# A two-layer graph kernel: where the bias of v, the scaling of the sums, layer 1's first sums and the key loads stand in the order of the work

## The chip, the cores and the metric

The kernel runs on one core of a Trainium2 chip. The metric is the device time in microseconds (us). TensorE (PE in the profile) multiplies matrices, PEld is its weight load, VectorE is DVE, ScalarE is ACT, GpSimd is POOL, and SyncE (SP) issues transfers. A waiting instruction holds up everything behind it on its engine or queue.

## The reference, cut to what matters

There are 16 graphs (b) of 1024 nodes with 256 features. Layer 0 is masked attention with 8 heads of 32; layer 1 is a graph layer whose scores come from the layer's own input `h` and one of four vectors, chosen by the value of `adj`.

```python
h = relu(layernorm(x))
Q, K, V = h @ Wq.T + bq, h @ Wk.T + bk, h @ Wv.T + bv           # by heads
attn = softmax(where(adj == 0, -inf, Q @ K.T * HD ** -0.5))     # per head
x = x + (attn @ V) @ Wo.T + bo
h = relu(layernorm(x))
e_k = leaky_relu((h * a_k) @ h.T, 0.2)                          # k = 0 .. 3
scores = where(adj == k + 1, e_k, -9e15)                        # the kind chosen per edge
x = x + softmax(scores) @ h
```

The adjacency is drawn as 0 or 1, so only `a_0` is used at run time; a general path for other values stands behind a test at the end of the program.

## The kernel before, in words

The main loop has 138 steps `s`; a step handles one tile of 128 nodes in several places at once. Attention of layer 0 works on tile `s` (`now`) and finishes tile `s - 1` (`was`); `gone` is the tile before. Normalising and projecting (`Piece`) runs nine tiles ahead: `piece_nxt` is loaded, `piece` is normed and turned, `piece_was` gets its keys, values and queries. Layer 1 (`Edges`) runs nine tiles behind: `edge` gets its scores, `edge_was` its sums and the store. Eight tiles make a graph; `t` is the tile within it, and between `t` = 7 and `t` = 0 the graph turns: the eight key tiles `k0` to `k7` (512 KB each) are loaded anew.

Each step runs over `h` = 0 to 7, and the order of the instructions on every engine is the order written in the program; no scheduler moves them. Waits are set from the data: an instruction waits for those that wrote what it reads or that still use what it overwrites, kept by whole tile. For head `h` a step has:

- scores(h), L423: TensorE writes a 128x1024 tile into one of two PSUM places.
- max(h), L435: VectorE adds the mask and finds the row's extreme; exp(h), L443, on ScalarE follows, issued in turn `h + 1`.
- The transpose of the probabilities, issued in turn `h + 2`. Heads 2, 3, 6, 7: TensorE, L543, with copies by ScalarE, L544. Heads 0, 1, 4, 5: VectorE turns blocks of 32x32 (L364, `turn_blocks`), then SP issues four transfers that put the blocks in place (L369, `place_blocks`). So head 1 is turned in turn h = 3, without TensorE.
- combine(0) in h = 7 and combine(1) in h = 3 of the next step, L478: TensorE sums the values over heads 0 to 3 and 4 to 7. combine(0) needs the transfers of heads 0 and 1, combine(1) those of heads 4 and 5.

The change and its surroundings touch these:

- L328 (`values`, h = 2) multiplies for v; L339 (`biased`) adds its bias on VectorE.
- L488 (`combined`): oT, the sums times the reciprocals, on VectorE. L493 (`output`, h = 4): TensorE multiplies oT by Wo. L499 (`residual`, h = 5): VectorE adds x.
- L231 (`piece.turn`, h = 5): TensorE transposes the next tile's h; L243 and L244 (`turned`): ScalarE copies it to SBUF. L261: the projections; L277 (`high`, ScalarE) and L282 (`split`, VectorE) read them in two parts and write `halves`, which go to DRAM as keys (kd, L309) and queries (qd, L303).
- L565: layer 1's scores; L579: their maximum on VectorE. L609 (`gather`): layer 1's sums, the first half in h = 5, the second in h = 6, from pT1, which comes through L364 and L369 as well. L618 (`store`): VectorE scales them and adds x, SP writes them out.
- L394 (`load`, h = 4): the adjacency of the tile after next, 512 KB, on the POOL queue. L403 makes the mask from it.
- L344 (`load_key`): one key tile, on the POOL queue. `KEY_STEPS` says where: entry i is the place of key i, 2h for the start of turn h and 2h + 1 for its end, in the step `t` = 7, and over 15 in the next one.

Two PSUM banks serve most of this. `sums_place` and `brief` lie in the first, `early` and `late` in the second. v's product, the query and key projections, `output` and the turn of h all go through `early` and `late`; since waits are kept by whole tile, a reader of one half of a bank also waits for the last write to the other half. So L277 for the queries waits for L231 if L231 was issued before it. combine, gather and `store` share `sums_place`, so combine(0) waits for L618.

SP issues its transfers one at a time and marks their ends in eight semaphores, its lanes, taken in turn: a transfer waits until the one before it on its lane, eight transfers earlier, has landed.

The lines that fix the order of keys and of h = 5 are these:

```python
KEY_STEPS = (6, 10, 13, 15, 18, 20, 22, 24)
...
(nc.sync, nc.gpsimd)[b > 0].dma_start(out=kt.bitcast(F32), in_=kds[b][c, ...])
```

Of the kernel before, what the change touches and what calls it, by code (L numbers as in the profile page):

```python
# [42 lines left out]
def gnn_kernel(  # L43
# [26 lines left out]
    LEAD = NT + 1  # L70


    KEY_STEPS = (6, 10, 13, 15, 18, 20, 22, 24)
    KEPT = LAG + 1

    const = ctx.enter_context(tc.tile_pool(name="const", bufs=1))
# [264 lines left out]
    def load_key(b, h):  # L341
        kt = keys.tile([P, N], F32R, tag=f"k{h}", name=f"k{h}_{b}")
        c, r = divmod(h, GROUP)
        (nc.sync, nc.gpsimd)[b > 0].dma_start(  # L344
            out=kt.bitcast(F32),
            in_=kds[b][c, r * HD : (r + 1) * HD].rearrange("d w u n -> (d w u) n"),
        )
        keysets.setdefault(b, {})[h] = kt
# [178 lines left out]
    def norms(tile_0, piece):  # L527

        both = [(a, x) for a, x in ((tile_0, tile_0 and tile_0.x1), (piece, piece and piece.x[:, 0, :])) if a]
        if both:  # L530
            mv = stats_place(len(both))
            for i, (_, xt) in enumerate(both):
                stats_of(xt, mv[:, i, :])
            r, shift = norm_of(mv)
            for i, (a, _) in enumerate(both):
                a.norm = r[:, i : i + 1], shift[:, i : i + 1]
# [151 lines left out]
    def attend_of(s):  # L688
        return Attend(*divmod(s, NT)) if 0 <= s < B * NT else None

    def edges_of(s):
        s -= LAG
        return Edges(*divmod(s, NT)) if 0 <= s < B * NT else None

    def piece_of(s):
        s += LEAD
        return Piece(*divmod(s, NT)) if s < B * NT else None

    with tc.manual_schedule():
        first = [Piece(0, 0, 4), Piece(0, 4, 4)]  # L700
        piece_was = Piece(1, 0)
# [23 lines left out]
        piece, edge, edge_was = piece_next, None, None  # L725
# [10 lines left out]
        for s in range(B * NT + LAG + 1):  # L736
            b, t = divmod(s, NT)

            def load_keys(h, end):
                if t == NT - 1 and b + 1 < B and 2 * h + end in KEY_STEPS:  # L740
                    load_key(b + 1, KEY_STEPS.index(2 * h + end))
                if t == 0 and 0 < b < B and 2 * (HEADS + h) + end in KEY_STEPS:
                    load_key(b, KEY_STEPS.index(2 * (HEADS + h) + end))

            nxt2, edge_nxt, piece_nxt = attend_of(s + 2), edges_of(s + 1), piece_of(s + 1)
            for h in range(HEADS):
                ending, eh = (now, h - 1) if h >= 1 else (was, HEADS - 1)
                turning, th = (now, h - 2) if h >= 2 else (was, HEADS + h - 2)

                load_keys(h, 0)  # L750


                if now:
                    now.scores(h)
                if h == 0 and piece_was:
                    piece_was.split()
                if h == 1 and piece_was:
                    piece_was.split()
                if h == 2 and edge:
                    edge.softmax_max()  # L760
                if h == 4 and piece_was:
                    piece_was.biased()
                if h == 4 and was:
                    was.combined()
                if h == 5:
                    if was:
                        was.residual()
                    norms(was, piece_nxt)
                if h == 6 and edge_was:
                    edge_was.gather(1)  # L770
                if h == 6 and piece_was:
                    piece_was.split()
                    piece_was.split()
                if now:
                    now.softmax_max(h)
                if h == 6 and edge_was:
                    edge_was.store()
                if h == 4 and edge:
                    edge.leak()


                if ending:
                    ending.softmax_exp(eh)

                if h == 1 and gone:
                    gone.turned_normed()


                if turning and th in BY_BLOCKS:
                    turning.turn_blocks(th)  # L790
                    turning.place_blocks(th)
                elif turning:
                    turning.turn(th, 0)
                    turning.turn(th, 1)


                if h == 0:
                    if piece_was:
                        piece_was.write_again()
                    if edge:  # L800
                        edge.score(0)
                    if gone:
                        gone.turn_normed()
                    if edge_was:
                        edge_was.turn_blocks()
                        edge_was.place_blocks()
                if h == 1:
                    if edge:
                        edge.score(1)
                    if was:  # L810
                        was.reciprocals()
                    if piece_nxt:
                        piece_nxt.load()
                    if piece_was:
                        piece_was.write_again()
                    if nxt:
                        nxt.load_queries()
                if h == 2:
                    if piece_was:
                        piece_was.values()  # L820
                    if was:
                        was.turn_reciprocals()
                        was.turned_reciprocals()
                        was.add_bias()
                    if edge_was:
                        edge_was.load_nodes()
                if h == 3:
                    if piece_was:
                        piece_was.project(1, 0)
                        piece_was.project(1, 1)  # L830
                    if was:
                        was.combine(1)
                    if nxt:
                        nxt.flag()
                        nxt.mask()
                if h == 4:
                    if was:
                        was.output()
                    if piece:
                        piece.normed()  # L840
                    if edge_nxt:
                        edge_nxt.prepare()
                    if nxt2:
                        nxt2.load()
                if h == 5:
                    if piece:
                        piece.turn()
                    if edge_was:
                        edge_was.gather(0)
                    if piece_was:  # L850
                        piece_was.high()
                        piece_was.high()
                    if piece:
                        piece.turned()
                if h == 6:
                    if edge:
                        edge.softmax_exp()
                    if was:
                        was.keep()
                    if now:  # L860
                        now.load_nodes()
                    if piece:
                        piece.project(0, 0)
                        piece.project(0, 1)
                if h == 7:
                    if now:
                        now.combine(0)
                    if piece_was:
                        piece_was.write_queries()
                    if piece:  # L870
                        piece.high()
                        piece.high()
                    if was:
                        was.normed()
                load_keys(h, 1)
            gone, was, now, nxt = was, now, nxt, nxt2
            edge_was, edge = edge, edge_nxt
            piece_was, piece = piece, piece_nxt
# [52 lines left out]
```

## Time and profile before

| what | value |
|---|---|
| median of 3 runs | 3343.77 us (3342.66 to 3351.56) |
| the profiled execution | 3346.32 us |
| its span, first to last instruction | 3344.4 us |
| mean granted TensorE clock | 0.985 |
| busy: TensorE, VectorE, ScalarE, GpSimd | 3091.6, 2809.3, 2466.1, 1726.9 us |
| TensorE waits for oT (L493 <- L488) | 75.6 us in 119 places |
| TensorE waits for the residual (L231 <- L499) | 26.6 us in 109 places |
| TensorE's combine waits for transfers of pT | 44.1 us in 32 places |
| transfers of pT, issue to landing, median | 3.5 us |
| key loads from POOL, issue to landing, median | 6.9 us |

A line of the timeline has the start in us, the length in us, the engine, the line of the kernel, the operation, out<-in, shapes and count; in brackets stands how long the engine was idle before it and what released it. "POOL L344 DMA_DIRECT2D" is the issue of a transfer on the POOL queue, not its movement. A line of stretches has the bounds, the length, busy time with the number of instructions of each engine, the granted TensorE clock, the mean busy share of the DMA engines and the GB/s they moved.

### The profile page before, as it was taken

The numbers are of one execution on the slowest core, as the hardware profiler recorded it, in microseconds if no ns is written. First come the engines' busy times: TensorE is split into PE (matmuls) and PEld (weight loads), VectorE is DVE, ScalarE is ACT, GpSimd is POOL, SyncE is SP. The second block draws the span as 40 slices with busy tenths as digits, with TensorE's granted clock in tenths as the row PEclk, the third lists the DMA queues.
The fourth block names the chain that finished last, engine by engine and source line by source line (L and its number), as shares of the span: only waits on it lengthen the run. The fifth ranks groups of instructions, "written<-read, shape, count | busy, mean of one in ns | idle before, by whom it ended". The sixth has DMA issues, their size and how long they took to land. (4 is left out here: it accounts for less than half of the span.)

```text
span 3344.4 us, 98033 instructions
## 1 busy us (share of the span) xinstructions
PE 3091.6 (92%) x36018; PEld 2217.5 (66%) x36018; DVE 2809.3 (84%) x5111; ACT 2466.1 (74%) x4829; POOL 1726.9 (52%) x3902
## 2 busy tenths in 40 slices
PE   4888999999999999999999999999999999999997
PEld 2766667676676666667667676666666676676653
DVE  2888889889888888888889888888888888888873
ACT  2887777777777777777777777777778778777750
POOL 2555555555555555555545555555555555555431
PEclk7999999999999999999999999999999999999999
DMA  5777787877878787787877878787787877877642
GB/s 191 227 229 247 214 263 228 256 223 227 252 221 267 212 244 241 213 257 231 256 218 229 255 223 269 217 246 239 215 266 222 260 224 231 249 228 236 192 136 70
DMA packets 747063, 762.93 MB, mean 228 GB/s; under 512 B 71280, under 2 KB 692080, under 8 KB 746576
## 3 DMA queue, kind: packets, MB, share of 16 engines
q1 hardware_dynamic: 678288, 542.21, 54.4%
q0 software_dynamic: 65088, 210.16, 20.1%
q8 instruction: 290, 4.75, 0.6%
q10 hardware_dynamic: 3200, 4.19, 0.3%
q14 instruction: 197, 1.61, 0.1%
HBM read 252.98 MB, written 167.77 MB: 126 GB/s over the span
## 5 line engine op out<-in xcount | busy, mean ns | idle before, releaser
L443 ACT ACTIVATE p<-p,nmx 128x1024 f32<-128x1024 f32 x1024 | 1178.0, 1150 | 308.4 <-DVE nmx L435 304.4
L435 DVE CUSTOM_DVE_ANT_0 p<-s,neg 128x1024 f32<-128x1024 f32 x1024 | 1235.1, 1206 | 140.4 <-issue 69.3
L423 PE MATMUL s<-k,qt 128*128 128x512 f32 x2048 | 794.5, 469 | 16.1 <-DVE nmx L435 9.5
L403 POOL TENSOR_SCALAR neg<-adj 128x1024 bf16<-128x1024 int32 x128 | 466.7, 3646 | 361.7 <-ACT neg L415 361.5
L544 ACT COPY pT<-trp 128x512 f32<-128x512 f32 x1024 | 544.3, 582 | 141.0 <-PE trp L543 125.0
L364 DVE STREAM_TRANSPOSE blocks<-p 128x1024 f32<-128x1024 f32 x512 | 633.2, 1237 | 0.1
L478 PE MATMUL acc<-pT,v 128*32 128x128 f32 x16384 | 529.1, 277 | 45.1 <-DMA pT<-blocks 44.1
L543 PE MATMUL trp<-ident,p 128*128 128x128 f32 x4096 | 530.9, 273 | 0.0
L478 PEld LDWEIGHTS acc<-pT,v 128*32 128x32 f32 x16384 | 448.8, 111 | 121.6 <-issue 94.9
L543 PEld LDWEIGHTS trp<-ident,p 128*128 128x128 f32 x4096 | 479.0, 140 | 69.4 <-issue 0.8
L609 PE MATMUL acc<-h,pT 128*32 128x256 f32 x8192 | 509.6, 383 | 12.2 <-DMA pT<-blocks 11.9
L565 PE MATMUL s<-h1T,ha 128*128 128x512 f32 x1024 | 481.6, 594 | 0.5 <-ACT h1T L522 0.5
L423 PEld LDWEIGHTS s<-k,qt 128*128 128x128 f32 x2048 | 329.3, 191 | 190.2 <-issue 154.7
L609 PEld LDWEIGHTS acc<-h,pT 128*32 128x32 f32 x8192 | 246.0, 110 | 227.7 <-issue 70.5
L462 POOL COPY wide<-rec 128x256 f32<-128x256 f32 x128 | 50.8, 397 | 556.1 <-DVE rec L460 556.1
L309 POOL DMA_DIRECT2D kd<-halves x240 | 168.3, 701 | 310.7 <-DVE halves L282 297.4
L579 DVE CUSTOM_DVE_ANT_0 sel<-s,neg 128x1024 f32<-128x1024 f32 x128 | 156.8, 1225 | 145.1 <-PE s L565 145.1
L565 PEld LDWEIGHTS s<-h1T,ha 128*128 128x128 f32 x1024 | 175.1, 190 | 129.7 <-issue 128.4
L493 PE MATMUL acc<-woT,oT 128*128 128x256 f32 x512 | 143.9, 403 | 75.6 <-DVE oT L488 75.6
L591 ACT ACTIVATE sel<-sel,nmx 128x1024 f32<-128x1024 f32 x128 | 145.2, 1134 | 69.3 <-DVE rec L616 64.0
L443 ACT ACTIVATION_READ_ACCUMULATOR p<-p,nmx 128x1 f32 x1024 | 193.2, 189 | 0.0
L472 ACT COPY recT<-acc 128x256 f32<-128x256 f32 x128 | 47.7, 373 | 178.1 <-PE acc L468 178.1
(106 smaller groups left out, 3986.7 us busy)
## 6 DMA issues: line engine op xcount, KB each, us to landing
pT<-blocks SPq DMA_DIRECT2D x2560, 128.0 KB, 3.5
qt<-qd SPq DMA_DIRECT2D x128, 512.0 KB, 5.6
adj<-in_adj POOLq DMA_DIRECT2D x127, 512.0 KB, 4.8
qd<-halves SPq DMA_DIRECT2D x240, 256.0 KB, 2.9
k<-kd POOLq DMA_DIRECT2D x120, 512.0 KB, 6.8
kd<-halves SPq DMA_DIRECT2D x240, 128.0 KB, 3.7
kd<-halves POOLq DMA_DIRECT2D x240, 128.0 KB, 3.6
xb<-in_x POOLq DMA_DIRECT2D x128, 128.0 KB, 2.6
```

What stands on the lines that cost most here:

```text
L309: queue.dma_start(out=kds[self.b][oc, :, :, twice, self.cols], in_=halves.rearrange("p (w n) -> p w n", w=2),)
L364: nc.vector.transpose(blocks.rearrange("p b j q -> p j b q"), p)
L403: nc.gpsimd.tensor_scalar(self.neg, self.adj, 0.0, MASKED, ALU.is_equal, ALU.mult)
L423: nc.tensor.matmul(self.ps[:, cols], lhsT=self.qt[:, h, :], rhs=keysets[self.b][h][:, cols], start=True, stop=True,)
L435: nc.vector.tensor_tensor_reduce(out=p, in0=sides[h in (3, 5, 7)], in1=self.neg, scale=-SCALE, scalar=FLOOR, op0=ALU.add, op1=ALU.min, acc ...
L443: nc.scalar.activation(p, p, AF.Exp, bias=nmx, scale=-1.0, accum_out=self.sums[:, h : h + 1])
L478: nc.tensor.matmul(sums_place[r * HD : (r + 1) * HD, g * P : (g + 1) * P], lhsT=vs[self.b][:, j, place_of(h) : place_of(h) + HD], rhs=self ...
L543: nc.tensor.transpose(tr[:, j, :], p[:, jj * P : (jj + 1) * P], ident)
L544: copy(pT[:, half * 4 : half * 4 + 4, :], tr)
L565: nc.tensor.matmul(self.e[:, cols], lhsT=self.ha[:, c, :], rhs=h1Ts[self.b][:, c, cols], start=(c == 0), stop=(c == NC - 1),)
L579: nc.vector.tensor_tensor_reduce(out=self.sel, in0=self.e, in1=masks[self.b, self.t], scale=-1.0, scalar=3e38, op0=ALU.add, op1=ALU.min, a ...
L609: nc.tensor.matmul(sums_place[a * HD : (a + 1) * HD, :], lhsT=self.pT[:, j, a], rhs=h1s[self.b][:, j, :], start=(j == 0), stop=(j == NT - 1),)
```

## The change

Four things move; no instruction is added or taken away.

1. The second, third, fourth and fifth key are loaded at other places: `KEY_STEPS` 10, 13, 15, 18 become 9, 10, 13, 16. Entry 9 (the end of h = 4) and entry 10 (the start of h = 5) have the same neighbours on the POOL queue for the key at that place.
2. project(1, .) and combine(1) are written ahead of the turn of head 1 in h = 3. Head 1's turn has nothing on TensorE, so TensorE's order stays.
3. The bias of v and oT go from h = 4, ahead of max(4), to h = 3, ahead of head 1's block transpose; on VectorE the order max(3), transpose, bias, oT, max(4) becomes max(3), bias, oT, transpose, max(4).
4. In h = 5 the first half of layer 1's sums (gather(0)) goes ahead of the turn of h on TensorE.

On POOL the order in the step `t` = 7 was: adjacency, key 1, the norm, xb, keys 2 and 3, kd, key 4. It becomes: adjacency, keys 1 and 2, the norm, xb, keys 3 and 4, kd. ScalarE's order and SP's order do not change.

```diff
-    KEY_STEPS = (6, 10, 13, 15, 18, 20, 22, 24)
+    KEY_STEPS = (6, 9, 10, 13, 16, 20, 22, 24)
...
-                if h == 4 and piece_was:
-                    piece_was.biased()
-                if h == 4 and was:
-                    was.combined()
                 if h == 5:
                     if was:
                         was.residual()
...
+                if h == 3:
+                    if piece_was:
+                        piece_was.project(1, 0)
+                        piece_was.project(1, 1)
+                    if was:
+                        was.combine(1)
+                    if piece_was:
+                        piece_was.biased()
+                    if was:
+                        was.combined()
                 if turning and th in BY_BLOCKS:
                     turning.turn_blocks(th)
                     turning.place_blocks(th)
...
                 if h == 3:
-                    if piece_was:
-                        piece_was.project(1, 0)
-                        piece_was.project(1, 1)
-                    if was:
-                        was.combine(1)
                     if nxt:
                         nxt.flag()
                         nxt.mask()
...
                 if h == 5:
+                    if edge_was:
+                        edge_was.gather(0)
                     if piece:
                         piece.turn()
-                    if edge_was:
-                        edge_was.gather(0)
                     if piece_was:
                         piece_was.high()
                         piece_was.high()
```

## The prediction

> **What bounds the kernel now.** I read the busy shares first, then the busy time by stretch, then the timeline of one ordinary step on all engines, and last the waits of TensorE and the POOL queue in a step where the graph turns.
>
> ```profile
> span 3344.4 us, 98033 instructions
> PE 3091.6 (92%) x36018; PEld 2217.5 (66%) x36018; DVE 2809.3 (84%) x5111; ACT 2466.1 (74%) x4829; POOL 1726.9 (52%) x3902
> ```
>
> No engine is full: TensorE leaves 8%, VectorE 16%. From the starts of scores(0) in the trace, 84 ordinary steps (t = 1 to 6, with layer 1 running) last 24.41 us in the median, 24.46 in the mean; the 14 steps with t = 7 last 26.9 in the mean, the steps with t = 0 after them 26.4. The stretches below are an ordinary step, a step t = 7 and the t = 0 after it (the last two columns are DMA share and GB/s).
>
> ```profile
> core 0: us, PE busy (x) PEld busy (x) DVE busy (x) ACT busy (x) POOL busy (x), PEclk, DMA share, GB/s
> 1498.98:1523.40 24.42, 23.59 (x286) 17.11 (x282) 21.89 (x41) 19.28 (x39) 12.95 (x29) 1.00 0.77 221
> ...
> 1419.93:1447.11 27.18, 23.99 (x286) 17.26 (x283) 22.75 (x42) 20.21 (x40) 16.32 (x35) 1.00 0.85 255
> 1447.11:1474.58 27.47, 24.87 (x285) 17.50 (x282) 22.25 (x40) 19.39 (x38) 14.15 (x32) 1.00 0.96 304
> ```
>
> TensorE is idle for 0.83 us of the ordinary 24.42, VectorE for 2.5: between them they form a ring, in which each waits for the other once or more. The timeline of that step shows where:
>
> ```profile
> 1505.62 1.23 DVE L579 CUSTOM_DVE_ANT_0 sel<-s,neg 128x1024 f32<-128x1024 f32 x1 [1.04 <-PE s L565]
> ...
> 1508.46 1.95 PE L478 MATMUL acc<-pT,v 128*32 128x128 f32 x64
> ...
> 1509.48 1.18 DVE L435 CUSTOM_DVE_ANT_0 p<-s,neg 128x1024 f32<-128x1024 f32 x1
> ...
> 1510.60 1.24 DVE L364 STREAM_TRANSPOSE blocks<-p 128x1024 f32<-128x1024 f32 x1
> ...
> 1511.77 0.38 DVE L339 TENSOR_TENSOR v<-acc,bv_t 128x256 f32<-128x256 f32 x1
> ...
> 1512.07 0.40 DVE L488 TENSOR_TENSOR oT<-acc,recT 128x256 f32<-128x256 f32 x1
> ...
> 1512.53 1.13 PE L493 MATMUL acc<-woT,oT 128*128 128x256 f32 x4 [0.58 <-DVE oT L488]
> ...
> 1515.24 0.41 PE L231 MATMUL acc<-ident,h 128*128 128x128 f32 x2 [0.25 <-DVE x L499]
> 1515.58 1.93 PE L609 MATMUL acc<-h,pT 128*32 128x256 f32 x32
> ...
> 1520.11 0.48 DVE L618 SCALAR_TENSOR_TENSOR ot<-acc,rec,x 128x256 f32<-128x256 f32 x1 [0.59 <-PE acc L609]
> ```
>
> combine(1) (L478) is over at 1510.41, yet oT comes 1.66 us later, since the block transpose of head 1 stands ahead of it on VectorE. TensorE has its transposes of head 2 behind it at 1511.95 and waits 0.58 for oT; after scores(5) and the transposes of head 3 it waits 0.25 for the residual (L499), which the turn of h (L231) may not overtake in their common bank. These two are all of TensorE's idle time in the step. VectorE's waits (1.04, 0.59 and two of some 0.3) are for TensorE.
>
> In the step t = 7, TensorE waits for a transfer, and the POOL queue shows what moved at that time:
>
> ```profile
> 1442.45 0.41 PE L478 MATMUL acc<-pT,v 128*32 128x128 f32 x2
> 1445.23 1.95 PE L478 MATMUL acc<-pT,v 128*32 128x128 f32 x62 [2.38 <-DMA pT<-blocks]
> ```
>
> ```profile
> 1436.54 0.61 POOL L394 DMA_DIRECT2D adj<-in_adj  x1
> 1437.15 0.53 POOL L344 DMA_DIRECT2D k<-kd  x1
> 1442.72 0.59 POOL L400 DMA_DIRECT2D xb<-in_x  x1
> 1443.31 1.07 POOL L344 DMA_DIRECT2D k<-kd  x2
> ```
>
> **The change, part by part.** [...]TensorE's order differs in one place alone (gather(0) ahead of the turn of h): project(1, .) and combine(1) followed scores(3) before too, since head 1 is turned by VectorE and DMA. So "in front of head 1's turn" acts on VectorE only.
>
> *Bias and scaling ahead of the transpose.* VectorE: max(3) lets the next instruction start at 1510.60. The bias takes that place, oT follows 0.30 later as before, at 1510.90 (combine(1) is over at 1510.41: no new wait, 0.5 us in hand), and ends at 1511.30. The transpose starts at 1511.24 instead of 1510.60, max(4) at 1512.41 as now: VectorE's sum is the same. L493 starts at 1511.95 instead of 1512.53: **-0.58**. Behind the transpose that is 0.64 later, SP has the four copies of head 1's blocks; they are the last four of eight that SP issues one by one from 1511.49, and their turn comes near 1514.5, two microseconds after the transpose's new end. Cost nothing by SP's backlog; if that were gone, up to 0.64 on the landing.
>
> *gather(0) ahead of the turn of h.* It waits for nothing that is late (its pT1 landed over 3 us before in ordinary steps), and starts at 1514.99 - 0.58 = 1514.41. The turn of h comes after its 1.86 us, at 1516.27; the residual has been there since 1515.09, so the 0.25 is gone. scores(6) starts at 1516.61 instead of 1517.44: **-0.83** in all. What is late instead: ACT's four readings of that bank (both L277 for the queries, L243, L244) start when L231 is over, near 1516.73 instead of 1515.81, so +0.92. VectorE's L282, which waits for L244, goes from 1517.34 to 1517.93, and max(6) from 1518.22 (it waited 0.28 there) to 1518.46. The store L618 waited 0.59 for gather(1), which now ends at 1519.21, so it starts near 1519.85, 0.26 earlier than now. combine(0), at 1520.69, needs it ended: 1520.33, 0.36 in hand. exp(5) on ACT is 0.36 late, and ACT idles 0.69 ahead of exp(7). So the 0.92 is paid from waits that exist, and the ring closes through TensorE: L579, which waits 1.04 today, is released 0.83 earlier and still waits.
>
> *Transfers that now come too late.* combine(0) needs head 1's four copies, and the adjacency load (512 KB, L394) is issued at about the same moment as the last of them. With combine(0) 0.83 earlier, the landings of the 84 ordinary steps as they stand would be later than it in 39% of them, by 0.26 us in the mean (now 15% and 0.05). That is +0.21. An ordinary step gains 0.83 - 0.21 = 0.62: 84 x 0.62 = **-52 us**. The seven steps at the end without projections wait 0.93 for oT each; I take 0.7 of it: **-5**. The nine steps before layer 1 begins show no such wait (L493 started without idle time): 0.
>
> *The key loads.* Key 1 keeps its place in the POOL queue (after the adjacency load, ahead of the norm). Key 2 moves from behind xb (1443.31) to right behind key 1, some 1437.7; key 3 takes key 2's place, and key 4 goes from 1446.26, behind kd, to right behind key 3, some 1443.85. The norm on POOL is 0.53 later in that step, so is layer 1's norm on ACT: a step that waits for a transfer anyway. The last copy of head 1's blocks was issued at 1438.0 and took 7.0 to land (L369 in that window); adj took 6.8 from 1436.5, key 1 7.5 from 1437.2. So they landed at 1443.3, 1444.7 and 1445.0: the copy right behind the loads issued before it, and so in each of the 14 turns, 0.2 to 0.5 behind key 1 whether it was issued at 17.4 or at 20.1 us of the step. By this row, key 2, ahead of it now, puts it off by the distance of two loads (1.3 here, 1.5 in the mean): combine(0) **+1.5 per turn** of 14, and the 0.83 is not had there. [...] I take the row. The next step, t = 0, has its DMA engines 96% busy; keys 2 to 4 all landed in it. With key 2 out of the way and key 4 issued 2.4 earlier, SP's waits for lanes there go, TensorE's wait for pT1 (up to 1.2) and most of that ahead of combine(0) too. I put t = 0 at 23.6 and 1.1 for adj against the blocks: 24.7 instead of 26.4, **-1.7**. A turn is thus -0.2, 14 of them **-3**; from -1.7 by the rule (-24) to +2.3 if key 2 costs 2.3, the longest distance seen, and t = 0 returns nothing (+32).
>
> Sum: -52 - 5 - 3 = -60. The profiled execution took 3346.3 (span 3344.4 and 1.9 around it), 2.5 above the median of 3343.8; 3346.3 - 60 = 3286, against the median **3284**.
>
> **The rivals.** *Slower: the late turn of h on ACT and VectorE.* L231 is now followed, over ACT, by VectorE's L282, max(6), the store, and combine(0). I find 0.36 of slack at the last. If ACT's four readings come more than 0.92 + 0.36 = 1.28 late (ACT is still busy with the copies of head 3 until 1515.92, and exp(5) stands behind), each further 0.1 us costs 11 us over 110 steps; past 1.0 more the gain of 0.62 is gone. If nothing absorbed L282's +0.59, the step would be 25.0: 110 x 0.59 = +65, **3409**. Against it: VectorE has 2.5 idle in the step, 0.87 of it just there. *The turn of the graph eats it.* If key 2 costs 2.3 and the next step gives nothing: -57 + 32 = -25, **3319**; for it, the share of 96%; against it, DMA fell to 117 GB/s between key 1 and key 2 before, room that key 2 fills. [...]*No effect*: transfers hold the ring at its period, since SP's copies start from head 4's transpose of the step before: **3344**; against it, 61% of the landings are early enough.
>
> **How the numbers follow.** The forecast has 0.68 (its own range 3262 to 3308), the eaten gain 0.12, the round-robin case 0.06, no effect 0.05, slower 0.09. What a measurement of this kernel tells from no change is about 0.3%, 10 us. The range 3250 to 3335 leaves out the slower case, most of no effect and the end of the best one. Faster by over 0.3%: 0.86; within: 0.05; slower: 0.09.
>
> **What would show it.** Right: L493 without idle time before it, L231 too, ordinary steps of 23.6 to 24.0, L579 and L618 still waiting; combine(0) waiting for pT in more steps than now and for some 4 us at t = 7, and t = 0 near 24.7. Wrong: oT waiting for L478; L478 waiting for the store L618; L282 followed by a TensorE wait; ordinary steps still at 24.4; keys that scores (L423) wait for.

## The result and the profile after

| | before | after |
|---|---|---|
| median of 4 runs each, us | 3346.73 (3342.66 to 3351.56) | 3295.86 (3285.52 to 3310.77) |
| ratio, 95% interval | | 0.9853 (0.9815 to 0.9892) |
| the profiled execution, us | 3346.32 | 3310.77 |
| 84 ordinary steps: median, mean, shortest | 24.41, 24.46, 23.96 | 23.75, 23.86, 23.16 |
| 14 steps t = 7, 14 steps t = 0: means | 26.95, 26.20 | 29.29, 24.68 |

The change makes the kernel 51 us faster in the medians; 3284 had been forecast. The profiled execution of after is the slowest of its four runs, so its sum is 15 us above its median; what single profiles say of the turns is held against the medians below. The step times are taken from the starts of scores(0) in the trace. The page of after begins so:

```profile
span 3309.0 us, 98026 instructions
PE 3080.0 (93%) x36018; PEld 2239.0 (68%) x36018; DVE 2802.7 (85%) x5111; ACT 2458.4 (74%) x4829; POOL 1735.3 (52%) x3902
```

The groups of TensorE (line, engine, operation, count | busy, mean ns of one | idle just before, by releaser) show where its idle time went:

```profile
L478 PE MATMUL acc<-pT,v 128*32 128x128 f32 x16384 | 561.0, 283 | 112.3 <-DMA pT<-blocks 110.7 <-ACT recT L472 0.5 <-issue 0.4
...
L493 PE MATMUL acc<-woT,oT 128*128 128x256 f32 x512 | 133.6, 383 | 0.6 <-DVE oT L488 0.6
L231 PE MATMUL acc<-ident,h 128*128 128x128 f32 x240 | 52.2, 299 | 1.6 <-DVE x L499 1.1 <-DVE v L339 0.5
```

Both waits that the change was to remove are gone: L493's 75.6 us and L231's 26.6 us became 0.6 and 1.1. But combine's wait for transfers of pT (L478) rose from 44.1 us to 110.7. Two thirds of what was freed there stands in front of another instruction.

An ordinary step without a wait, start and length first, on TensorE and VectorE:

```profile
1361.74 1.23 DVE L579 CUSTOM_DVE_ANT_0 sel<-s,neg 128x1024 f32<-128x1024 f32 x1 [1.04 <-PE s L565]
...
1366.71 0.41 DVE L339 TENSOR_TENSOR v<-acc,bv_t 128x256 f32<-128x256 f32 x1
1367.05 0.41 DVE L488 TENSOR_TENSOR oT<-acc,recT 128x256 f32<-128x256 f32 x1
1367.38 1.23 DVE L364 STREAM_TRANSPOSE blocks<-p 128x1024 f32<-128x1024 f32 x1
...
1367.91 1.03 PE L493 MATMUL acc<-woT,oT 128*128 128x256 f32 x4
...
1370.20 1.93 PE L609 MATMUL acc<-h,pT 128*32 128x256 f32 x32
1372.07 0.44 PE L231 MATMUL acc<-ident,h 128*128 128x128 f32 x2
1372.26 0.71 PE L423 MATMUL s<-k,qt 128*128 128x512 f32 x2
...
1375.65 0.48 DVE L618 SCALAR_TENSOR_TENSOR ot<-acc,rec,x 128x256 f32<-128x256 f32 x1
```

oT now stands ahead of the transpose of head 1, L493 starts without idle time, the first half of L609 runs ahead of L231, and L618 no longer waits (0.59 before). The maximum of layer 1 (L579) waits 1.04 as before. The stretches show such a step beside its neighbour with a wait, then a turn (t = 7, t = 0):

```profile
1330.82:1355.11 24.29, 23.50 (x285) 17.22 (x282) 22.39 (x41) 19.82 (x39) 13.02 (x29) 1.00 0.78 228
1355.11:1378.28 23.17, 23.17 (x285) 17.12 (x283) 20.82 (x39) 18.39 (x38) 13.01 (x29) 1.00 0.75 228
1402.11:1432.51 30.40, 25.21 (x286) 18.72 (x283) 22.80 (x42) 20.00 (x40) 16.40 (x35) 0.89 0.91 281
1432.51:1456.74 24.23, 23.60 (x285) 17.03 (x282) 21.55 (x39) 18.40 (x37) 14.01 (x31) 1.00 0.84 267
```

In the second line TensorE is busy for all of the 23.17 us: in this step it is the bound. In the first line it is idle for 0.79, and one wait holds all of it. The step is longer by more than that, and 0.34 of it is combine(0) itself: two of its 64 matmuls run ahead of the wait, and the two parts take 0.41 and 1.95 us where the 64 in one row take 2.02; the last line is combine(0) of the second step, without a wait:

```profile
1352.04 0.41 PE L478 MATMUL acc<-pT,v 128*32 128x128 f32 x2
1353.23 1.95 PE L478 MATMUL acc<-pT,v 128*32 128x128 f32 x62 [0.79 <-DMA pT<-blocks]
...
1376.33 2.02 PE L478 MATMUL acc<-pT,v 128*32 128x128 f32 x64
```

In the turn, the same wait is longer, and the matmuls behind it are slower (3.63 us for the 62 instead of 1.95). POOL's queue shows keys 1 and 2 issued together right behind the adjacency load, and keys 3 and 4 behind xb:

```profile
1428.95 3.63 PE L478 MATMUL acc<-pT,v 128*32 128x128 f32 x62 [5.19 <-DMA pT<-blocks]
```

```profile
1418.76 0.61 POOL L394 DMA_DIRECT2D adj<-in_adj  x1
1419.37 1.05 POOL L344 DMA_DIRECT2D k<-kd  x2
...
1425.48 0.60 POOL L400 DMA_DIRECT2D xb<-in_x  x1
1426.08 1.07 POOL L344 DMA_DIRECT2D k<-kd  x2
```

Where the 35.6 us between the two profiled executions come from, by steps: ordinary steps -50.3 (84 x 0.60), the 28 steps of the turns +11.4, the last steps without projections (121 to 126) -5.9, step 8 (the second of the first turn) +6.3, the steps before it +1.7. That makes -36.8; the other 1.2 lie outside these steps.

### The profile page after: what moved, and what is told of

Same layout as the page of the kernel before. It is cut to its first block, busy times and chain, and to the rows that moved or that the text cites. A ratio compares the mean times of both kernels' runs of the same rounds, so it can differ in the third digit from the quotient of the medians.

```text
span 3309.0 us, 98026 instructions
## 1 busy us (share of the span) xinstructions
PE 3080.0 (93%) x36018; PEld 2239.0 (68%) x36018; DVE 2802.7 (85%) x5111; ACT 2458.4 (74%) x4829; POOL 1735.3 (52%) x3902
## 5 line engine op out<-in xcount | busy, mean ns | idle before, releaser
L478 PE MATMUL acc<-pT,v 128*32 128x128 f32 x16384 | 561.0, 283 | 112.3 <-DMA pT<-blocks 110.7
L478 PEld LDWEIGHTS acc<-pT,v 128*32 128x32 f32 x16384 | 472.1, 114 | 196.8 <-issue 119.4
L609 PE MATMUL acc<-h,pT 128*32 128x256 f32 x8192 | 509.9, 383 | 12.5 <-DMA pT<-blocks 11.8
L609 PEld LDWEIGHTS acc<-h,pT 128*32 128x32 f32 x8192 | 246.6, 110 | 228.5 <-issue 78.0
L579 DVE CUSTOM_DVE_ANT_0 sel<-s,neg 128x1024 f32<-128x1024 f32 x128 | 156.8, 1225 | 146.2 <-PE s L565 146.2
L261 PEld LDWEIGHTS acc<-hT,wkT 128*128 128x128 f32 x960 | 119.5, 195 | 76.1 <-issue 46.9
```

Of the source, the lines that this page charges most:

```text
L478: nc.tensor.matmul(sums_place[r * HD : (r + 1) * HD, g * P : (g + 1) * P], lhsT=vs[self.b][:, j, place_of(h) : place_of(h) + HD], rhs=self ...
L579: nc.vector.tensor_tensor_reduce(out=self.sel, in0=self.e, in1=masks[self.b, self.t], scale=-1.0, scalar=3e38, op0=ALU.add, op1=ALU.min, a ...
L609: nc.tensor.matmul(sums_place[a * HD : (a + 1) * HD, :], lhsT=self.pT[:, j, a], rhs=h1s[self.b][:, j, :], start=(j == 0), stop=(j == NT - 1),)
```

## The experiments

Twelve kernels ran; each ratio is to runs of the kernel before on the same chip. The runs stand on several chips, so two kernels are compared here by how far each lies under the kernel before on its own chip.

### The parts of the change, one at a time

e1: only the bias and the scaling in front of head 1's transpose.

```diff
-                if h == 4 and piece_was:
-                    piece_was.biased()
-                if h == 4 and was:
-                    was.combined()
...
+                if h == 3:
+                    if piece_was:
+                        piece_was.project(1, 0)
+                        piece_was.project(1, 1)
+                    if was:
+                        was.combine(1)
+                    if piece_was:
+                        piece_was.biased()
+                    if was:
+                        was.combined()
...
                 if h == 3:
-                    if piece_was:
-                        piece_was.project(1, 0)
-                        piece_was.project(1, 1)
-                    if was:
-                        was.combine(1)
```

> Only the bias of v and oT go ahead of head 1's block transpose (with project(1, .) and combine(1) written ahead of it); key loads and gather(0) stay as before. Theory A, the ring: oT (L488) comes 1.2 us earlier and L493 starts without a wait, but the residual (L499) stands behind max(4) and the leak on VectorE, whose times don't move, and the turn of h (L231) still stands ahead of gather(0): TensorE waits some 1.0 us there in place of 0.58 + 0.25. Ordinary steps stay at 24.4, and the time within 8 us of before (3344). Theory B, the parts add up: L493's 0.58 to 0.84 are gained alone, ordinary steps 23.6 to 23.8, some 45 us faster (3300).

Measured: 3348.16 against 3350.72, ratio 0.9988 (0.9979 to 0.9997). So theory A was right. Its ordinary steps last 24.41 in the median, as before. The groups of TensorE in this kernel say why:

```profile
L493 PE MATMUL acc<-woT,oT 128*128 128x256 f32 x512 | 132.8, 382 | 0.6 <-DVE oT L488 0.6
L231 PE MATMUL acc<-ident,h 128*128 128x128 f32 x240 | 49.0, 286 | 121.7 <-DVE x L499 120.1 <-ACT p L443 1.1 <-DVE v L339 0.5
```

The 75 us in front of L493 are gone, and 94 more stand in front of L231: TensorE is earlier there, and the residual (L499) that the turn of h waits for is not, since VectorE's order behind the transpose is what it was. The wait has moved by one instruction, and the part alone is worth next to nothing. What it gains lies in the last steps without projections (121 to 126), which are 5.4 us shorter than before.

e2: only gather(0) in front of the turn of h.

```diff
                 if h == 5:
+                    if edge_was:
+                        edge_was.gather(0)
                     if piece:
                         piece.turn()
-                    if edge_was:
-                        edge_was.gather(0)
```

> Only gather(0) ahead of the turn of h; the rest as before. Theory A: L493 still waits 0.58 for oT; the turn of h has its residual in time, and the pair gather(0), turn of h, scores(6) is some 0.2 shorter in this order, so 0.45 us per ordinary step: 23.95, 84 x 0.45 = 38 less, minus up to 10 for head 1's copies that now land too late: 3306 to 3316. Theory B: the 0.25 alone, 84 x 0.25 = 21 less: 3323. Rival: the later reading of the bank by ScalarE and VectorE (L277, L282) costs what is gained: 3344 or more.

Measured: 3343.47, ratio 0.9979 (0.9967 to 0.9991): 7 us, less than either theory expected and the number of the rival. Its groups:

```profile
L478 PE MATMUL acc<-pT,v 128*32 128x128 f32 x16384 | 543.8, 278 | 61.4 <-DMA pT<-blocks 60.4 <-ACT recT L472 0.5 <-issue 0.3
...
L493 PE MATMUL acc<-woT,oT 128*128 128x256 f32 x512 | 143.9, 403 | 75.9 <-DVE oT L488 75.9
L231 PE MATMUL acc<-ident,h 128*128 128x128 f32 x240 | 52.1, 299 | 0.8 <-DVE v L339 0.5 <-DVE x L499 0.2
```

L231's wait is gone, L493's stays, and 16 us have gone over to L478. The mechanism was theory A's and not the rival's: ordinary steps without a wait for copies last 24.02 in the median, 0.39 less than before. But 25 of the 84 now wait for copies (14.6 us), their mean is 24.33 (24.46 before), and the 28 steps of the turns are 4.7 us longer. So most of what the order gains here is lost to transfers that land too late, and the rest of the ring's 1.25 us is not to be had while L493 still waits.

e3: only the new places of the keys.

```diff
-    KEY_STEPS = (6, 10, 13, 15, 18, 20, 22, 24)
+    KEY_STEPS = (6, 9, 10, 13, 16, 20, 22, 24)
```

> Only the new KEY_STEPS. Theory C, a copy lands behind every load issued before it: combine(0) at t = 7 waits some 1.5 to 2.5 us longer (3.5 to 5 us in all), t = 0 is 1.5 shorter, the first turn (steps 7 and 8, without layer 1) some 6 longer: 3344 to 3365. [...]

Measured: 3356.94, ratio 1.0021 (1.0010 to 1.0032): 6 us slower. In its profile t = 7 lasts 27.82 instead of 26.95, t = 0 25.99 instead of 26.20, the 28 steps together 9.3 us more. The time is in theory C's range; but t = 7 grew by 0.9 where C had 1.5 to 2.5, and t = 0 fell by 0.2 where C had 1.5.

e4: the whole change, with the keys at their old places.

```diff
-    KEY_STEPS = (6, 9, 10, 13, 16, 20, 22, 24)
+    KEY_STEPS = (6, 10, 13, 15, 18, 20, 22, 24)
```

> The changed kernel with the old KEY_STEPS. Theory C: t = 7 back to some 27, t = 0 to some 26, the first turn (step 8) back to 24: 10 to 20 us below the changed kernel, 3276 to 3286. [...]Ordinary steps as in the changed kernel, 23.9 in the mean, 23.2 where no copy is late.

Measured: 3295.80, ratio 0.9839 (0.9817 to 0.9862), so within its interval no slower than the kernel after. In its profile t = 7 is 26.19, t = 0 is 26.87, the 28 steps together 742.8 us, where the kernel after has 755.5 and before had 744.1. The ordinary steps are those of the kernel after (23.88 in the mean). Theory C had expected 10 to 20 us less than the kernel after, and 24 for step 8, the second of the first turn, which took 31.53. The new key places cost the turns some 9 to 13 us by the profiles of e3 and e4, and 6 and 4 us by the medians (the 4 within the noise).

The four together: bias and scaling alone are worth some 3 us, gather(0) alone 7, the two in one kernel 55 (e4). The gain belongs to the pair.

### What takes part of the ring's gain back

In the kernel after, 41 of 84 ordinary steps wait for head 1's copies in combine(0), 35 us in all; before, 3 did, 0.6 us in all. e5 moves the load of the adjacency tile (L394, 512 KB), which was issued 16.6 us into the step at about the time of the last copy, behind the loads of h = 6, 23 us into it.

```diff
                 if h == 4:
...
-                    if nxt2:
-                        nxt2.load()
...
                     if now:
                         now.load_nodes()
+                    if nxt2:
+                        nxt2.load()
```

> The changed kernel with the adjacency load (L394) moved from h = 4 to h = 6, behind xb on the POOL queue. Theory E: what takes back the ring's gain in ordinary steps is head 1's last copy landing behind this 512 KB load. Then combine(0) waits no more in ordinary steps: all of them near 23.2, 84 x 0.65 = 55 less than the changed kernel; at t = 7 the copy has 512 KB less ahead of it, 1.3 us per turn or 18 in all: 3215 to 3250. Theory F: the copy is late since SP's own backlog, begun by head 4's transpose, doesn't shrink with the step: the waits stay, ordinary steps 23.9 in the mean, 3285 to 3300.

Measured: 3258.33, ratio 0.9714 (0.9688 to 0.9740). Ordinary steps last 23.19 in the median, and these waits fell from 35 to 4 us; t = 7 waits for 51 us still. The groups and the stretch of three such steps in a row:

```profile
L478 PE MATMUL acc<-pT,v 128*32 128x128 f32 x16384 | 551.3, 282 | 67.4 <-DMA pT<-blocks 66.5 <-ACT recT L472 0.5
```

```profile
1439.10:1462.27 23.17, 23.17 (x286) 17.12 (x282) 21.25 (x39) 18.82 (x38) 12.62 (x29) 1.00 0.77 233
1462.27:1485.45 23.18, 23.18 (x285) 17.14 (x282) 21.72 (x41) 19.23 (x38) 13.09 (x30) 1.00 0.78 234
1485.45:1508.64 23.19, 23.19 (x285) 17.13 (x282) 21.72 (x41) 19.23 (x38) 13.10 (x30) 1.00 0.76 233
```

TensorE has no idle time left in them. The cause of the waits in ordinary steps is shown: the load that is issued about when the copies are, not a backlog of SP's queue, whose order the edit does not touch. By the traces the last copy is even issued later than in the kernel after (17.8 us into the step instead of 16.9, in the median), but it lands after 2.65 us instead of 4.44. In total this is 43 us under the kernel after, less than expected (3215 to 3250): the ordinary steps gained 0.47 in the mean and not 0.65, and the turns (28.44 and 24.70) 11.5 us in all and not 18.

e6: e5 with the keys at their old places (both edits above).

> The same with the old KEY_STEPS. Theory E: ordinary steps 23.2; at t = 7 only key 1 is ahead of head 1's last copy, so some 0.5 to 1.5 us less there than with the new places: 3205 to 3245. If the key places matter only through this copy, the difference to the kernel with the new places is under 15 us. Theory F: 3275 to 3295.

Measured: 3248.53, ratio 0.9689 (0.9667 to 0.9711). This is the fastest version together with e11 below, some 53 us under the kernel after, though a little short of the 3205 to 3245 expected. The wait of L478 is

```profile
L478 PE MATMUL acc<-pT,v 128*32 128x128 f32 x16384 | 545.6, 279 | 56.3 <-DMA pT<-blocks 53.9 <-DVE blocks L364 1.1 <-ACT recT L472 0.5
```

and the 28 steps of the turns last 733.7 us, where e5 has 744.0. By the medians this is 10 us under e5, a third measure of what the new key places cost.

e7: e5 with only key 0 in front of the adjacency load, the others in h = 6 and later.

```diff
-    KEY_STEPS = (6, 9, 10, 13, 16, 20, 22, 24)
+    KEY_STEPS = (6, 12, 13, 16, 18, 20, 22, 24)
```

> The adjacency load at h = 6 and KEY_STEPS (6, 12, 13, 16, 18, 20, 22, 24): keys 1 and 2 behind the norm, so that only key 0 is ahead of head 1's copies. Theory C (a copy lands behind every load issued before it): combine(0) at t = 7 waits under 1 us, step t = 7 some 23.5 to 24.5; keys 1 to 4 now pile up in t = 0 and scores(1) or combine(1) wait there 1 to 3 us: t = 0 27 to 29. In all within 20 us of the kernel before it in this list: 3210 to 3250. [...]

Measured: 3268.56, ratio 0.9745 (0.9718 to 0.9772), slower than e6. t = 7 falls to 24.10 with waits of 8.6 us in 14 turns, as theory C had it, and t = 0 rises to 29.90, more than it had (27 to 29), so that the total lies above its range (3210 to 3250): what the keys no longer take in one step they take in the next.

e8: the late adjacency load alone, on the kernel before (the edit of e5).

> The kernel before with the adjacency load at h = 6 alone. Theory E: in the ring of before combine(0) waits only 0.05 us in ordinary steps, so they stay at 24.41; t = 7 gains up to 1.3 per turn, 18 in all: 3325 to 3345. If the late load helped by itself (on VectorE or POOL), ordinary steps would be under 24.3 and the time under 3320.

Measured: 3338.33, ratio 0.9949 (0.9930 to 0.9969). Ordinary steps stay at 24.40, t = 7 falls by 1.9 and t = 0 rises by 1.7. So the late load is worth 14 us where the ring is slow, and 43 us (e5 against the kernel after) where it is fast.

### The slow matmuls of the turn

In the kernel after, 11 of the 14 waits at t = 7 are followed by a combine of 2.8 to 3.6 us instead of 1.95, 17.3 us too much in all; before, 3 were, with 3.4 us. The stretches of one such wait, with PEclk as the third number from the end:

```profile
1423.40:1424.40 1.00, 0.36 (x3) 0.09 (x2) 1.00 (x2) 1.00 (x4) 0.74 (x4) 1.00 1.03 419
1424.40:1425.40 1.00, 0.00 (x0) 0.00 (x0) 1.00 (x3) 0.25 (x1) 0.69 (x4) 1.00 1.01 395
1425.40:1426.40 1.00, 0.00 (x0) 0.00 (x0) 1.00 (x3) 0.81 (x2) 1.00 (x3) 0.71 0.98 333
...
1430.95:1431.95 1.00, 1.00 (x27) 1.00 (x21) 0.00 (x0) 0.00 (x0) 0.00 (x0) 0.50 0.86 292
1431.95:1432.95 1.00, 1.00 (x12) 0.57 (x6) 0.00 (x0) 0.00 (x0) 0.00 (x0) 0.65 0.98 371
1432.95:1433.95 1.00, 1.00 (x10) 0.91 (x9) 0.53 (x1) 0.19 (x1) 0.00 (x0) 1.00 1.07 382
```

TensorE stops at 1423.76; some 2 us later the granted clock falls from 1.00 to 0.50, and it stays so through the wait and the whole combine, from 1425.8 to 1432.6. To see what that costs, e9 keeps TensorE at work during the wait: matmuls over heads 2 and 3, whose sums combine(0) then writes over.

```diff
+        def fill(self):
+            for j in range(NT):
+                for r in (2, 3):
+                    nc.tensor.matmul(
+                        sums_place[r * HD : (r + 1) * HD, 0:P],
+                        lhsT=vs[self.b][:, j, place_of(r) : place_of(r) + HD],
+                        rhs=self.turned[r][:, j],
+                        start=(j == 0),
+                        stop=(j == NT - 1),
+                    )
...
+                    if now and s % NT == NT - 1 and NT < s < 15 * NT:
+                        for _ in range(3):
+                            now.fill()
```

> The kernel after, with filling work on TensorE in the 14 turn steps t = 7: ahead of combine(0) come three passes over heads 2 and 3 of its own sums (their probabilities are there since h = 5), 16 matmuls each, an estimated 2.9 us of work (half of combine's 1.95 us for 64 matmuls of four heads at a time gives 0.98 a pass); combine(0) then writes over these sums. Nothing else changes. In the kernel after, TensorE waits 2.5 to 6.0 us there, and in 11 of 14 turns the matmuls of combine(0) that follow take 2.8 to 3.6 us instead of 1.95, 17.3 us in all (3.4 in the kernel before), with a granted clock of 0.50. Theory G, the clock is the term that I left out of the turn: filled, TensorE is idle for at most 3.1 us in one piece, most of these stretches keep the full clock, and t = 7 falls from 29.3 to some 28.3: about 14 us less than the kernel after, near 3282, ratio 0.981 (0.979 to 0.983). Theory H, the landing of the transfers alone sets the turn and what follows it (the slow matmuls are paid from a wait of the next step): no change, 3296, ratio 0.985, or a few us more where the wait was shorter than the filling.

Measured: 3304.35, ratio 0.9866 (0.9848 to 0.9884). A pass took 1.8 us, not 0.98 (L489: 76.1 us for three passes in 14 steps), so the filling ran past the landing in 11 of 14 turns. The clock was never halved at t = 7 (a matmul of L478 takes 277 ns in the mean of this profile, 283 in that of the kernel after). t = 7 fell to 28.44, near what the theory of the clock had, but t = 0 rose to 25.29, and the ratio is that of theory H.

e10: four passes (`range(4)`).

> The same with four passes, an estimated 3.9 us: longer than the wait in 4 of the 14 turns (by 0.4 to 1.4 us, 3.7 in all), and idle for at most 2.1 us in the others. Theory G: the clock never drops at t = 7, 17 less 4: about 12 to 13 us less than the kernel after, near 3283, ratio 0.9815. Theory H: 3300, ratio 0.986.

Measured: 3315.35, ratio 0.9894 (0.9875 to 0.9912). The filling, 7.2 us long, is now itself the end of t = 7 (30.07), so the time lies above the numbers of both theories.

e11: one pass, in the version e6.

> One pass of the same filling, an estimated 0.98 us, in the version with the adjacency load at h = 6 and the keys at their old places (ratio 0.969). There TensorE waits 0.5 to 2.5 us in these turns, and 4 of 14 have slow matmuls, 5.2 us in all. Theory G: 4 to 5 us less than that version, near 3244, ratio 0.9676. Theory H: as it was, 0.969, or 0.5 us more for the one turn with a wait of 0.5.

Measured: 3243.48, ratio 0.9696 (0.9682 to 0.9710), the same as e6's 0.9689 within the intervals. In its profile the clock is not halved at t = 7 (a matmul of L478 takes 275 ns in the mean, 279 in e6), and the 28 steps last 724.9 us instead of 733.7; but that profile is of the fastest of its five runs, and the medians do not tell the two versions apart.

e12: two passes in the kernel after, 3.7 us, shorter than most of its waits.

> The kernel after with two passes of the filling in the 14 turn steps t = 7. A pass measured 1.8 us with three of them (76.1 us for L489 in 14 steps), not the 0.98 that I had estimated, so three passes took 5.4 us and ran past the landing in 10 of 14 turns; two take 3.6, shorter than the wait of the kernel after in 11 of 14 turns. With three, the clock stayed full at t = 7, yet t = 7 fell by 0.85 and t = 0 rose by 0.6, in sum 3 us in 14 turns. Theory G, the halved clock costs about 1 us a turn and three passes hid that by their own length: with two, combine(0) takes 1.95 after its wait, t = 7 near 28.1, t = 0 near 24.7 as in the kernel after, t = 7 and t = 0 together near 52.8 instead of 53.97; near 3282, ratio 0.981. Theory H, the pair of steps is set by its transfers, and what t = 7 saves t = 0 gives back, waiting for keys and blocks: the pair near 53.7, 3293 to 3304, ratio 0.984 to 0.987.

Measured: 3297.68, ratio 0.9853 (0.9832 to 0.9874), that of the kernel after. The page's group for the filling, and the stretches of a turn:

```profile
L489 PE MATMUL acc<-pT,v 128*32 128x128 f32 x896 | 51.6, 273 | 0.0
```

```profile
1405.61:1432.32 26.71, 26.71 (x350) 20.51 (x347) 22.40 (x42) 19.59 (x40) 16.38 (x35) 1.00 0.91 281
1432.32:1458.45 26.13, 24.50 (x286) 17.36 (x283) 22.10 (x40) 19.06 (x38) 14.00 (x31) 1.00 0.91 293
```

t = 7 lasts 27.96 in the mean, 1.33 less than in the kernel after, and t = 0 25.78, 1.10 more: there TensorE waits 0.75 a turn for keys in front of scores (0.34 in the kernel after) and 0.89 for blocks in front of combine and gather (0.37). The pair is 53.74, as the theory of the transfers had it (53.7), not 52.8. Not all of the 1.33 is the clock's. Some 0.8 of it is that head 1's copies landed earlier in this execution (25.11 us of the step instead of 25.93), which the filling does not explain. The other 0.5 is left of the clock's part: combine(0) is slow in 3 turns instead of 11, but in 6 turns the filling ran past the landing. So the halved clock is real and lengthens t = 7, by 1.0 us a turn in the profile of the kernel after; but the kernel's time does not hang on it, since taking most of it away left the ratio at 0.9853.

## Why the prediction was right, point by point

*Ordinary steps, -0.62 each, 84 x 0.62 = -52.* Measured -0.60 and -50.3. The mechanism held, but that the number did is luck: the gain was larger than forecast, and two losses were larger by as much. The ring's gain was put at 0.83, and a step without waits gained 1.25 in the median (24.41 to 23.16). In the medians of the trace L493 starts 0.74 earlier (I had 0.58) and is 0.10 shorter (1.03 instead of 1.13); the gap ahead of L231 gave 0.25 as said; and scores(6) starts 0.19 after the turn of h, where I had let it wait for 0.34. Against that, the lateness of transfers was put at 0.21 a step and is 0.42 in the mean (35.1 us in 84 steps). I had moved combine(0) by 0.83 against landings that stayed; moved by 1.29, as the trace has it (22.52 to 21.23 us into the step), it meets more of them: 0.39 in the mean with the landings of before. A term that I had put at nothing is combine(0) itself: with a wait behind its first two matmuls it is busy for 2.28 us, and in the mean of the 84 steps it takes 2.16 where it took 1.93. So 1.25 - 0.42 - 0.23 = 0.60. e5 shows the mechanism: with the adjacency load behind the copies the median is 23.19.

*That the two moves add up as -0.58 and -0.25.* This holds only for the two together. e1 shows L493's 0.58 going to L231, and e2 that gather(0) ahead of the turn of h without the 0.58 is worth 7 us. The sum was right because both were in the change; the working did not say that neither stands alone.

*The late turn of h on ACT and VectorE costs nothing.* Right. The store, whose lead over combine(0) I had put at 0.36, is not waited for: combine waits for blocks (110.7 us), and L618 is not among the releasers that its group lists. L579 still waits 1.04. L618's own wait, which I expected to shrink from 0.59 to about 0.33, is gone in such a step. (A slip in the rival's sum: the gain of 0.62 is gone after 0.62 more of lateness, not 1.0.)

*The end, -5.* Measured -5.9 in steps 121 to 126.

*A turn, -0.2 and -3 in all.* This is the step that failed: the pair went from 53.15 to 53.97, +0.8 a turn and +11.4 in all. At t = 7 the size held and the picture behind it only in part. Over the 14 turns the last copy of head 1's blocks lands at 25.94 us of the step instead of 24.58, +1.36, where I had +1.5 from the row. But I had let the copy land right behind every load issued before it. In 11 turns it was issued behind key 2, and it landed 1.9 later than before; yet only in five of these did it land behind key 2 (by 0.1 to 0.3), and in six it landed 0.3 to 1.4 ahead of it. In the other three it was issued ahead of key 2, and landed 0.6 earlier. The row told the delay well, though not the order. The -1.7 a turn (-24) at one end of my range, and the case that had 0.06 with it, let key 2 cost the copy nothing; no run shows that term, and with the new key places the copy landed 1.36 later in the mean. What was left out is the halved clock: 17.3 less 3.4 us in 14 turns, +1.0 each, and 1.36 + 1.0 is the +2.34 of t = 7. The other half of the step, t = 0 at 24.7, was met (24.68), by luck: before it was 26.20 and not the 26.4 that I had read, and the key places alone bring it to 25.99 (e3). A reason that fits, though no run isolates it, is that the longer t = 7 gave the keys time to land: where t = 7 is shorter (e12), t = 0 is 25.8. So keys 2 and 4 out of the way are not worth 1.7 in themselves. Scores also wait for keys in 9 places, 6.7 us in all, which I had named as a sign against me; it is small. In the sum 0.2 was right neither in sign nor in size; the rival "the turn of the graph eats it" had +2.3 per turn, so the truth lies between the two.

*The first turn, 0.* Step 8 took 30.25 instead of 23.92. It took between 24.4 and 31.5 in the other profiles, and 24.44 in e9, which has the same order and keys there. It goes with waits for keys and blocks of several us and a mean granted clock of 0.77 in that step (0.93 before). What decides it from one execution to the next is left open; it is a part of what makes the profiled execution of after long.

*Sum.* -60 was forecast, and the medians differ by 51. The ordinary steps and the end came to -56.2 where -57 had been put, so what is missing lies in the turns. Put at -3, they are +11.4 in the profile, which is of the slowest of four executions; by the medians the new key places cost 6 us (e3), 4 us (e4, within the noise) and 10 us (e6 beside e5), which with -56 comes near the 51.

## What to carry to other kernels

When two waits lie one behind the other in the same ring, price them together: with one taken away here (e1), TensorE arrived earlier at the next and waited there instead (120.1 us in front of L231 where it had been 26.6), and the parts measured singly (3 us and 7) say nothing of the pair (55). After a ring has been made faster, look at what is issued just ahead of the transfers that now end it: here moving one 512 KB load by 6 us in its queue gave 43 us more. A step that is set by its transfers should be judged together with its neighbour: three ways of shortening t = 7 here (the late load in e8, late keys in e7, filling in e12) lengthened t = 0 by most of what they saved, or by more. Over the 14 profiles t = 7 lies between 24.1 and 30.1 us, and the pair between 51.8 and 54.4.

## What the runs showed of the hardware

- A small copy on SP's queue landed later where one more large load had been issued on POOL's queue before it, but did not always land behind that load. In the profile of the kernel before, at t = 7, the last 128 KB copy of head 1's blocks, issued behind the adjacency and key loads (512 KB each), landed 0.2 to 0.5 us behind key 1 in each of the 14 turns. In that of the kernel after, with key 2 ahead of it too in 11 of the 14, it took 7.1 us instead of 6.0 in the mean of all 14; of the 11 it landed 0.1 to 0.3 us behind key 2 in five, and ahead of it in six. Key 1 itself, which still stands ahead of key 2, took 7.4 us instead of 7.0. What makes the copy and the key slower is not shown by any run here.
- The granted TensorE clock was halved in some of the waits of this kernel, and the length of a wait alone did not tell in which. In the profile of the kernel after, every one of the 10 waits at t = 7 over 4 us was followed by a combine of 3.4 to 3.6 us instead of 1.95, one of 3.5 by 2.8, and the three of 2.5 to 3.1 by 1.95; but in that of the kernel before, waits of 1.99 and 2.14 us were followed by 2.67 and 2.92 (granted clock 0.50 from 843.3 to 844.7 us and from 2246.2 to 2248.1 us), and three of 2.5 to 2.6 by 1.95. The halved stretch above lasts from 1425.8 to 1432.6, 6.8 us. The 10 waits over 4 us cost TensorE 1.5 to 1.7 us each beyond their own length. What else decides it, no run isolates.
- Keeping the clock full by work in the wait is possible (mean granted clock 0.991 in e12 against 0.979), and brought nothing to this kernel's time (ratio 0.9853 for both).
